# Delta * u of a scan unit loaded in three transfers of twelve channels instead of six of six

## The chip, the cores and the metric

The kernel runs on one core of one Trainium2 chip. The metric is the device time of one execution in microseconds (us); the figure for the kernel before is the median of three runs.

## What is computed

The reference has four layers on an image batch `x` of shape (4, 64, 64, 96). Layers 0 and 1 are selective-scan layers (a state-space block with a 3x3 depthwise convolution), layers 2 and 3 are linear attention followed by a feed-forward net with an FP8/FP16 quantisation. The change lies in the scan of layers 0 and 1, which is this recurrence for each of 4 images, 4 scan directions `k`, 192 channels `e` and 16 states `n`, over 4096 positions:

```python
dA = jnp.exp(d[..., None] * A)                       # d = delta of this position, A = -exp(A_logs)
h  = dA * h + d[..., None] * b[:, :, None, :] * u[..., None]
y  = jnp.einsum('bken,bkn->bke', h, c)
```

`d * u` does not depend on the state `n`; `b` and `c` do not depend on the channel `e`. So a kernel that holds states on partitions must bring the same `d * u` to 16 partitions.

## The kernel before

Each scan layer is run for two image pairs, which makes four phases. A phase has three parts: `prepare` (normalisation, projection, convolution, and the inputs of the scan, written to DRAM), `scan_phase` (the recurrence), and `finish` (gate, norm and output projection), where `finish` of one phase runs beside `prepare` of the next. Layers 2 and 3 follow at the end.

**Layout of the scan.** The 128 partitions hold 8 (image, direction) groups times 16 states. Partition `p` belongs to quarter `p // 32` of the 32-partition quarters, to group `p // 4 % 8`, and within it to one of 4 states. The time axis is cut into 8 chunks of 512 positions (`NC`, `TC`), the channels into 16 blocks of 12 (`NEB`, `EB`). One chunk of one block is a *unit*: a tile `h` of 128 partitions x 12 channels x 512 positions in float32, four of which are in rotation (`bufs=4`). A phase has 128 units, in the order chunk by chunk and block by block, so that four phases have 512.

**What a unit needs.** `load` (L381) first issues `load_delta` (L371), which brings delta, split into three bfloat16 parts, into 24 partitions (`dlt`). Then `load_quarters` (L391) fills the tile `h` with delta * u, straight from DRAM: each of the 8 group rows is read four times (a broadcast of stride zero), once for each of the 4 states of a quarter. To feed four quarters there are two copies of the array `du` in DRAM. With `first` counting quarters, the three combinations in the loop of L387 are:

- `first=1, quarters=2`: the two middle quarters (64 partitions), from both copies. Below it is called **A**.
- `first=0, quarters=1`: the first quarter (32 partitions), from copy 0. Called **B**.
- `first=3, quarters=1`: the last quarter (32 partitions), from copy 1. Called **C**.

Each is issued twice, for channels 0 to 5 and for channels 6 to 11, so the order of a unit's transfers is dlt, A0, A1, B0, B1, C0, C1. A row of `du` is padded by two channels (`PITCH`), and the channels of a block lie one behind the other in it, so the source of one partition is one contiguous run of 6 x 512 x 4 = 12,288 bytes.

**What is done with it.** GpSimd multiplies `h` by `b`, three channels at a time (`times_b`, L403, four for a unit, begun half a unit ahead: `B_LEAD`). TensorE spreads delta to 128 partitions through a 0/1 matrix (`replicate`, L408), ScalarE takes the exponential of it in PSUM (`decay`, L414), VectorE runs the recurrence along time, one channel at a time (`scan`, L420, twelve for a unit, in place in `h`). One unit later TensorE contracts the states with `c` (`contract`, L432), ScalarE copies the result out of PSUM (`evict`, L449), and `store` (L457) writes it to DRAM with four small transfers (`y<-d`).

**Order.** The order on each engine in `scan_phase` is the order of the code (a manual schedule). All loads and stores of the scan are issued by SyncE (SP), one after another: at the end of unit `at` it issues the four stores of unit `at-1`, then in some units four small transfers of `b` or `c` (L344), then the load of unit `at+3` (L529 to L534). The waits are set by the framework. Every DMA takes one of eight completion semaphores in turn, and before it is issued SP waits until the DMA that used this semaphore before, eight DMAs back, has landed. An ordinary unit issues 11 DMAs (dlt, six of delta * u, four stores).

Of the kernel before, what the change touches and what calls it, by code (L numbers as in the profile page):

```python
# [32 lines left out]
EB = 12  # L33
# [47 lines left out]
class Consts:  # L81
# [3 lines left out]
    def load(self, pool, name, shape):  # L85
        t = pool.tile(shape, F32, name=name)
        self.nc.sync.dma_start(t, self.a[name])
        return t
# [39 lines left out]
class Scans:  # L128
# [19 lines left out]
    def prepare(self, ph):  # L148
# [16 lines left out]
        with self.tc.tile_pool(name="prep", bufs=1) as wp, self.tc.tile_pool(  # L165
# [3 lines left out]
            def load(name, shape, at=0):  # L169
                t = wp.tile([at + shape[0]] + shape[1:], F32, name=name)  # L170
                nc.sync.dma_start(t[at:], a[pre + name])
                return t

            xp = load("x_proj", [C, 2, 2, XD2])
            dt_w = load("dt_w", [XD2 - 2 * NS, 2, E], at=2 * NS)
            conv_b = load("conv_b", [C, 2])
            ds = load("Ds", [C, 2, K])
            dsum = wp.tile([C, 2], F32, name="dsum")
# [202 lines left out]
    def load(self, u):  # L381

        nc, ph = self.nc, u.ph
        u.h = self.units.tile([128, EB, TC], F32, name="h", bufs=4)
        self.load_delta(u)
        n = EB // 2
        for first, quarters in ((1, 2), (0, 1), (3, 1)):  # L387
            for e in range(0, EB, n):
                self.load_quarters(u, e, n, first, quarters)

    def load_quarters(self, u, e, n, first, quarters):  # L391

# [591 lines left out]
```

## Time and profile before

| quantity | value |
|---|---|
| median of 3 runs | 12483.71 us (12462.94 to 12492.15) |
| profiled execution, its own time | 12443.48 us |
| its span, first to last instruction | 12441.7 us |
| the four scan stretches, first to last scan instruction | 774.8 to 2684.3, 3613.3 to 5524.1, 6462.3 to 8374.4, 9306.6 to 11235.0 us |
| busy in the span: PE, VectorE, ScalarE, GpSimd | 81%, 75%, 58%, 59% |
| TensorE clock granted | 0.665 |

The profile is of one execution. A group of instructions is named by its line, engine, operation and tiles; behind the bar stand its busy time, the mean duration of one in ns, and the idle time of its engine just before it with what ended most of that. `SPq` is SyncE's queue; its entries are the issuing of DMAs, not the moving of the data. The data moves on 16 DMA engines, and the share that the profile gives is a mean over the 16.

### The profile page before, as it was taken

What the parts mean: (1) busy time and instruction counts of PE and PEld (TensorE: products, weight loads), DVE (VectorE), ACT (ScalarE), POOL (GpSimd) and SP (SyncE); (2) the same over time, 40 slices, a digit from 0 to 9 for tenths busy, and PEclk for the clock granted to TensorE, in tenths of its full rate; (3) what the DMA queues carried; (4) which work ended last, traced back from release to release, by engine and by line L of the source; (5) the groups of instructions that cost most, each with busy time, mean ns of one, the idle gap of its engine ahead of it and who ended that gap; (6) DMA issues with size and microseconds to landing.
All of it is one profiled execution on the core that took longest, in us unless ns stands there. A gap on an engine that the chain in (4) does not pass through costs nothing.

```text
span 12441.7 us, 340858 instructions
## 1 busy us (share of the span) xinstructions
PE 10107.0 (81%) x147008; PEld 4972.1 (40%) x147008; DVE 9376.9 (75%) x9235; ACT 7185.6 (58%) x11815; POOL 7386.0 (59%) x2316
## 2 busy tenths in 40 slices
PE   7758888879878888879878888888878888887777
PEld 2224444433334444433334444443334444444333
DVE  2479999963569999982469999992459999993567
ACT  2456666644456666653456666663446666662556
POOL 0159999950149998960139899880129989990000
PEclk8665565669675555659775656558776655557787
DMA  3567676754667676764566777664567666663110
GB/s 92 172 227 247 244 248 247 248 168 140 213 205 246 245 247 244 250 200 128 176 215 244 246 247 249 243 226 125 174 202 249 244 243 245 245 244 122 30 21 11
DMA packets 882704, 2491.45 MB, mean 200 GB/s; under 512 B 279058, under 2 KB 561840, under 8 KB 737456
## 3 DMA queue, kind: packets, MB, share of 16 engines
q1 hardware_dynamic: 552496, 2163.38, 50.6%
q10 hardware_dynamic: 328704, 306.26, 8.5%
q8 instruction: 1158, 18.97, 0.7%
q14 instruction: 346, 2.83, 0.1%
HBM read 1955.42 MB, written 513.80 MB: 198 GB/s over the span
## 4 chain that ended last, share of the span: by engine, by line
DMA 53%; PE 20%; SPq 8%; DVE 7%; ACT 4%; issue 4%; POOL 3%; ACTq 1%; POOLq 0%; DVEq 0%
DMA h<-du 47%; PE c L260 8%; SPq L396 7%; POOL h L406 3%; PE f L591 2%; DVE h L423 2%; PE d L306 2%; DMA yk<-y 1%; PE c L289 1%; PE f L600 1%; POOL parts L320 1%; PE f L682 1%; DMA du<-du_sb 1%; PE y L441 1%; DVE parts L321 1%
## 5 line engine op out<-in xcount | busy, mean ns | idle before, releaser
L406 POOL TENSOR_TENSOR h<-h,b 128x1536 f32<-128x1536 f32 x2048 | 7016.6, 3456 | 780.6 <-DMA h<-du 369.0
L423 DVE TENSOR_TENSOR_SCAN h<-a,carry,h 128x512 f32<-128x512 f32 x5376 | 6356.7, 1259 | 391.8 <-POOL h L406 360.9
L416 ACT ACTIVATE a<-a,a_col 128x512 f32<-128x512 f32 x6144 | 4030.3, 662 | 1966.6 <-PE a L412 1814.4
L441 PEld LDWEIGHTS y<-h,cw 128*32 128x32 f32 x131072 | 2886.3, 145 | 3597.6 <-issue 1606.1
L441 PE MATMUL y<-h,cw 128*32 128x48 f32 x131072 | 3702.1, 269 | 438.0 <-ACT a L416 216.9
L412 PE MATMUL a<-dlt,rep 24*128 24x512 bf16 x6144 | 3319.4, 551 | 884.8 <-DVE h L423 782.1
L320 POOL CAST parts<-dl 96x1024 bf16<-96x1024 f32 x256 | 341.3, 1348 | 3092.1 <-DVE dl L317 2785.6
L316 DVE TENSOR_TENSOR du_sb<-dl,xc 96x1024 f32<-96x1024 f32 x256 | 397.3, 1577 | 1296.2 <-ACT dl L314 1234.8
L453 ACT COPY d<-y 128x384 f32<-128x384 f32 x2048 | 979.6, 478 | 485.7 <-PE y L441 432.7
L260 PE MATMUL c<-xn,taps 96*96 96x512 f32 x2304 | 1034.1, 609 | 73.5 <-DVE xn L245 71.0
L423 DVE TENSOR_TENSOR_SCAN h<-a,h 128x512 f32<-128x512 f32 x768 | 869.6, 1201 | 189.0 <-ACT a L416 110.6
L412 PEld LDWEIGHTS <-rep 24*128 24x128 bf16 x6144 | 471.9, 101 | 903.6 <-issue 451.0
L306 PE MATMUL d<-xd,dt_w 7*96 7x512 f32 x1024 | 520.8, 859 | 254.9 <-ACT xd L292 225.6
L260 PEld LDWEIGHTS c<-xn,taps 96*96 96x96 f32 x2304 | 382.6, 167 | 707.5 <-issue 628.7
L823 POOL MEMSET tn<- 1x4096 f32 x8 | 27.8, 3506 | 865.0 <-PE pa L843 514.7
L267 ACT ACTIVATE xc<-c,conv_b 96x512 f32<-96x512 f32 x128 | 87.3, 682 | 718.1 <-PE c L260 633.2
L591 PE MATMUL f<-yk,perm 128*128 128x384 f32 x1024 | 415.9, 546 | 99.6 <-DMA yk<-y 88.8
L314 ACT ACTIVATE dl<-d 96x1024 f32<-96x1024 f32 x256 | 252.0, 1017 | 400.9 <-DMA delta<-parts 234.5
L321 DVE TENSOR_TENSOR parts<-dl,parts 96x1024 bf16<-96x1024 f32 x256 | 366.9, 1455 | 153.2 <-POOL parts L320 153.1
L289 PE MATMUL c<-xc,x_proj 96*103 96x512 f32 x512 | 420.2, 958 | 4.2 <-ACT xc L267 4.2
L306 PEld LDWEIGHTS d<-xd,dt_w 7*96 7x96 f32 x1024 | 151.7, 212 | 542.4 <-ACT xd L292 295.8
L360 ACT ACTIVATE cw<-c,gmask 128x256 f32<-128x256 f32 x512 | 287.9, 573 | 126.2 <-DMA h<-du 65.9
(114 smaller groups left out, 5650.6 us busy)
## 6 DMA issues: line engine op xcount, KB each, us to landing
h<-du SPq DMA_DIRECT2D x1024, 768.0 KB
h<-du SPq DMA_DIRECT2D x2048, 384.0 KB
delta<-parts ACTq DMA_DIRECT2D x512, 288.0 KB
dlt<-delta SPq DMA_DIRECT2D x512, 288.0 KB
du<-du_sb SPq DMA_DIRECT2D x256, 384.0 KB
du<-du_sb ACTq DMA_DIRECT2D x256, 384.0 KB
y<-d SPq DMA_DIRECT2D x2048, 48.0 KB
yk<-y SPq DMA_DIRECT2D x256, 384.0 KB
```

The lines of the kernel that those rows point to most:

```text
L260: nc.tensor.matmul(rows(ps[:C]), taps[:, tap, h * C : (h + 1) * C], xn[:, ROWS * c + dy : ROWS * (c + 1) + dy, dx : dx + HW], start=tap == ...
L289: nc.tensor.matmul(rows(ps[:XD2]), xp[:, k, h], u[:, h], start=h == 0, stop=h == 1)
L306: nc.tensor.matmul(ps[:, m], dt_w[part, k, m * C : (m + 1) * C], xd[part], start=True, stop=True)
L321: nc.vector.tensor_tensor(parts[:, 2], delta, parts[:, 1], ALU.subtract)
L396: self.nc.sync.dma_start(u.h[32 * first : 32 * (first + quarters), e : e + n].rearrange("p e t -> p (e t)"), source.rearrange("a g e t -> ...
L406: self.nc.gpsimd.tensor_tensor(h, h, b, ALU.mult)
L412: self.nc.tensor.matmul(u.a[n], rep, u.dl[:, n], start=True, stop=True)
L416: self.nc.scalar.activation(u.a[n], u.a[n], AF.Exp, scale=u.ph.a_col[:, at : at + 1])
L423: self.nc.vector.tensor_tensor_scan(u.h[:, n], u.a.pop(n), u.h[:, n], 0.0 if u.c == 0 else u.ph.carry[:, at : at + 1], ALU.mult, ALU.add,)
L441: self.nc.tensor.matmul(view(u.y[32 * j : 32 * j + 32], l2 * EB, (8 * EB, 4), (1, EB)), u.ph.cw[u.c][:, l1, 8 * j + l2], view(u.h, 64 * l1 ...
L453: self.nc.scalar.copy(u.d[:, :, :, l1], u.y[:, : 32 * EB].rearrange("p (t h x) -> p t h x", t=4, h=2))
L591: nc.tensor.matmul(ps[:, : 4 * C].rearrange("p (w v e) -> p w v e", w=4, v=nv), cst.perm[:, k], view(t, off, (sw if k < 2 else -sw, 4), (1 ...
```

## The change

The inner loop over halves of six channels goes, and `load_quarters` is called with all twelve channels at once. A unit's transfers are now dlt, A, B, C: three of delta * u with contiguous runs of 24,576 bytes, in place of six with runs of 12,288. The bytes, the partitions and the order of the quarters are the same. An ordinary unit now issues 8 DMAs. Nothing else differs in the code.

```diff
         u.h = self.units.tile([128, EB, TC], F32, name="h", bufs=4)
         self.load_delta(u)
-        n = EB // 2
         for first, quarters in ((1, 2), (0, 1), (3, 1)):
-            for e in range(0, EB, n):
-                self.load_quarters(u, e, n, first, quarters)
+            self.load_quarters(u, 0, EB, first, quarters)
```

`load_quarters(u, e, n, first, quarters)` itself is unchanged; it loads `n` channels from channel `e` on.

## The prediction

> **What bounds the kernel now.** I read the page's chain first, then the scan stretches by windows, then one stretch as a timeline and as a chain. The page says where to look:
>
> ```profile
> DMA h<-du 47%; PE c L260 8%; SPq L396 7%; POOL h L406 3%; PE f L591 2%; DVE h L423 2%; PE d L306 2%; DMA yk<-y 1%; PE c L289 1%; PE f L600 1%; POOL parts L320 1%; PE f L682 1%; DMA du<-du_sb 1%; PE y L441 1%; DVE parts L321 1%
> L406 POOL TENSOR_TENSOR h<-h,b 128x1536 f32<-128x1536 f32 x2048 | 7016.6, 3456 | 780.6 <-DMA h<-du 369.0
> L423 DVE TENSOR_TENSOR_SCAN h<-a,carry,h 128x512 f32<-128x512 f32 x5376 | 6356.7, 1259 | 391.8 <-POOL h L406 360.9
> ```
>
> More than half of the chain is this load and its issue; VectorE waits for GpSimd, GpSimd for the load. The windows of the first scan stretch:
>
> ```profile
> core 0: us, PE busy (x) PEld busy (x) DVE busy (x) ACT busy (x) POOL busy (x), PEclk, DMA share, GB/s
> 775.00:2684.00 1909.00, 1621.64 (x34042) 832.57 (x34041) 1805.52 (x1536) 1305.54 (x2268) 1740.52 (x508) 0.60 0.70 245
> ```
>
> VectorE is busy 1806 of 1909 us: about 103 us a phase are lost. DMA at 0.70 looks free; it isn't, as shown below. The timeline of VectorE in a steady stretch, and then the chain of waits there (start, us, what):
>
> ```profile
> 1534.08 14.21 DVE L423 TENSOR_TENSOR_SCAN h<-a,carry,h 128x512 f32<-128x512 f32 x12 [0.34 <-POOL h L406]
> 1548.71 14.21 DVE L423 TENSOR_TENSOR_SCAN h<-a,carry,h 128x512 f32<-128x512 f32 x12 [0.42 <-POOL h L406]
> ```
>
> ```profile
> 1520.83 12.44 DMA h<-du
> 1533.29 0.69 SPq L396
> ...
> 1535.42 12.72 DMA h<-du
> 1548.14 0.02 issue
> 1548.16 0.69 SPq L396
> ```
>
> A unit needs 14.21 us of VectorE but begins every 14.6 to 14.7 us. The chain repeats: C1 lands (1533.27), which lets SP issue B0 (eight DMAs on), three more issues, and C1 of the next unit lands at 1548.14. The waits of SP say the same:
>
> ```profile
> SPq L396 <- DMA h<-du: 2039.9, 1326, 4.0
> SPq L461 <- DMA h<-du: 633.0, 657, 2.8
> ```
>
> Is this loop a latency or a full resource? The trace's semaphore records, which have the landing of each DMA engine's share, answer it. A shows 16 landings, B and C show 8 and one at the issue. So B, C and dlt run on 8 engines only, the same ones; the other 8 carry halves of A and stores. In one unit the last landings are dlt 1550.75, A0 1552.35, A1 1554.21, B0 1556.04, B1 1557.88, C0 1559.73, C1 1562.88. Four packets of 12,288 B in 1.84 us is 461 ns each; the packet records have 462 ns. The loaded engines ("low eight") have no gap. Over 508 units the median of C1 to C1 is 14.72 us: stores and dlt 2.70, A0 1.60, A1 1.85, B0 1.85, B1 1.84, C0 1.85, C1 2.85. Only C1 is 1.0 us over its 1.85. It is then that the high eight start A0 of the next unit: A0 is issued 4.6 us before C1 lands, its packets start 1.2 us later, the high eight finish A0 at +1.1 and A1 at +3.2, taking 6.6 us for 8 packets that need 3.7. Where no A runs beside it (before a load of b or c) C1 takes 1.85. The two streams slow each other. So the bound is the low eight engines, 14.72 us a unit, of which some 1.2 us (1.0 in C1, about 0.2 in dlt and stores) is contention.
>
> [...]
>
> **The change, part by part.**
>
> *Longer packets.* Packet medians in steady scans: 768 B 36 ns, 2048 B 84 ns, 12,288 B 462 ns. The line through these is 8.6 ns + bytes / 27.1 per ns. A 24,576 B packet should take 914 ns in place of 924. A low engine carries 24 of the short ones a unit (8 of A, 8 of B, 8 of C), so 12 x 8.6 = 0.10 us go. Three completion writes fewer, about 10 ns each by the 4 B packets: 0.03. Together -0.14 us a unit (rounded up). No packet in this trace is over 16,384 B, so an unseen split could make it 0; the bounds are -0.14 and 0.
>
> *SP.* Three issues of 0.65 us fewer a unit. SP stands in waits, so this is worth nothing itself.
>
> *The semaphore waits move.* With 8 DMAs a unit and 8 semaphores, each waits for its own counterpart of the unit before: A for A, C for C. A is now held by the later of two things. First, SP's order: the last eviction of a unit starts 12.4 us after its first scan (1513.77 against 1501.35), four stores take 2.5 and dlt 0.7, and the scan starts 3.5 after C lands (one GpSimd multiply): 3.5 + 12.9 + 3.2 = 19.6 us after the landing of a unit three back, which is 2 x 14.7 - 19.6 = 9.8 us before C of the unit just ahead lands. Second, the landing of A ahead: 4 x 1.84 + 1.2 = 8.6 us before. So A is issued some 8.6 us before the landing of C where it was 4.6 us. The low eight have work queued either way and gain nothing.
>
> *Contention.* But the high eight now begin A at -7.4 and, at 6.6 us, end at -0.8: 2.9 us of it lie beside B and 3.7 beside C, none beside dlt and stores, which cost little. Before, 3.4 us lay beside C0 and C1. Price beside C: 1.0 / 3.4 = 0.3 us per us, hence 1.1. Price beside B: the trace has it only at each phase's start, where the third load follows at once. There A0 ran beside B0 (1.85, no loss) and A1 beside B1 (2.85, 3.45, 3.00, 2.40 in the four phases); over 8.1 us of A the units lost 1.4 on average, 0.17 per us. So 2.9 us cost 0 to 1.0. The new loss is 1.1 to 2.1; I take 1.6. Against 1.2 that is +0.4; the bounds are -0.2 (all at 0.17 per us and some relief from one start of A in place of two) and +0.9.
>
> *Later first multiply.* GpSimd's first multiply waited for C0 and now waits for all of C, 1.84 us later. Behind it stand its own three multiplies, then VectorE's scans, and one unit on TensorE's contraction. In a loop set by DMA rate this shifts the phase, once: 4 x 1.84 = +7 us. At a phase's start it is hidden: VectorE's first scan there waits 37.73 us for ScalarE, whose 16 weights wait for c behind this load.
>
> *Sum.* -0.14 + 0.38 = +0.24 us a unit, over 496 units (the first four of a phase are ahead of the DMA): +119, with the +7, +126 us on the profiled 12443.5 (span 12441.7 and 1.8 around it), 1.0%. The profiled execution is 40 us below the median shown; on the median the same ratio gives 12,610 us.
>
> The units in which four transfers of b or c stand before the load keep their gap of about 2.6 us: there the fourth still waits for the last C, before and after.
>
> **Rivals.** *Packets decide* (28%): contention stays at 1.2 us wherever A lies, as the phase starts suggest (1.4 in all). Then -0.14 x 496 + 7 = -62 us: 12,420. Against it: units where A0 was early by chance (issued 7 us ahead of C1's landing) have C0 at 3 to 4.3 and C1 at 2.8 to 3.7. For it: part of that is another delay, also seen without A (single transfers of 3.4), which itself makes A look early.
>
> *Contention eases* (7%): one long A per unit starts once, not twice, and the streams fall out of each other's way, as where A ran on all 16 from a standstill with packets back at 462 ns. The floor is VectorE's 14.21 us a unit: 0.5 us x 496 = -250, near 12,240.
>
> *No change that can be measured* (8%): the two terms cancel or the packets are split; 12,460 to 12,508.
>
> *Contention doubles* is the far end of my forecast: +0.9 - 0.14 = +0.76 us a unit, +380 us, 12,870.
>
> **How the numbers follow.** The forecast, more contention than the packets save, has 57%, its own range 12,510 to 12,870. Below it lie 12,420 with 28%, 12,240 with 7%, and no change with 8%. About 0.2% (25 us) is what a measurement of this kernel can tell from none. The range 12,360 to 12,850 leaves out the 7% and the far ends. Faster 0.35, same 0.08, slower 0.57.
>
> **What would show it.** In the profile after: 24,576 B packets near 914 ns on the quiet low eight; SP's waits for h<-du at L394 fall, because A is issued earlier; if I am right, B plus C take more than 8.4 us from A's landing to C's (the sum now: 1.85 + 1.84 + 1.85 + 2.85 = 8.4), stores plus dlt less than 2.7, and VectorE waits longer for GpSimd than 391.8 us. I am wrong if units begin every 14.6 us or less, or if A is still issued 4 to 5 us ahead of C's landing.

## The result, and the profile after

| | before | after |
|---|---|---|
| median of 4 runs each, us | 12480.49 (12462.94 to 12492.15) | 13659.6 (13646.34 to 13677.61) |
| ratio, 95% interval | | 1.0947 [1.0927, 1.0967] |
| span of the profiled execution | 12441.7 | 13675.8 |
| the four scan stretches | 1909.5, 1910.9, 1912.1, 1928.4 | 2237.3, 2225.6, 2211.9, 2205.7 |
| one unit, start to start (medians of the four stretches) | 14.64 to 14.81 | 17.27 to 17.54 |

The kernel became 9.5% slower. The forecast was 12,610 us with a range up to 12,850: the direction was right, the size was too small by a factor of nine (+126 us against some +1,180). The stretches add up to 8880.5 us against 7660.9, so 1219.6 of the 1234.1 us by which the span grew lie in the scan.

From the page of the kernel after, the chain by line and the groups of GpSimd and VectorE (busy, mean ns of one, then idle before it and what ended most of that):

```profile
DMA h<-du 54%; PE c L260 7%; DVE h L421 5%; PE f L589 2%; POOL h L404 2%; PE d L306 2%; DMA yk<-y 1%; PE c L289 1%; PE y L439 1%; DMA y<-d 1%; PE f L680 1%; PE f L669 1%; PE f L598 1%; POOL parts L320 1%; DMA delta<-parts 1%
L404 POOL TENSOR_TENSOR h<-h,b 128x1536 f32<-128x1536 f32 x2048 | 7003.2, 3451 | 2018.4 <-DMA h<-du 1159.2
L421 DVE TENSOR_TENSOR_SCAN h<-a,carry,h 128x512 f32<-128x512 f32 x5376 | 6360.6, 1260 | 1472.3 <-POOL h L404 1404.6
```

The work itself costs what it did: a scan takes 1260 ns (1259 before), a multiply 3451 (3456). Only the idle time grew, VectorE's from 391.8 to 1472.3 us and GpSimd's from 780.6 to 2018.4. The chain is the same load as before. It has lost `SPq` as a member, as the chain of waits in the steady stretch shows (start, us, what):

```profile
1509.17 18.04 DMA h<-du
1527.22 0.02 issue
1527.23 17.39 DMA h<-du
1544.63 0.02 issue
1544.64 17.30 DMA h<-du
```

C of a unit is issued when C of the unit before lands, and lands 17.3 us later. Nothing but transfers lies between. VectorE in the same stretch, as a timeline, stops before every unit:

```profile
1530.87 14.21 DVE L421 TENSOR_TENSOR_SCAN h<-a,carry,h 128x512 f32<-128x512 f32 x12 [3.88 <-POOL h L404]
1548.28 14.21 DVE L421 TENSOR_TENSOR_SCAN h<-a,carry,h 128x512 f32<-128x512 f32 x12 [3.21 <-ACT d L451]
1565.59 14.21 DVE L421 TENSOR_TENSOR_SCAN h<-a,carry,h 128x512 f32<-128x512 f32 x12 [3.10 <-POOL h L404]
```

The stops were 0.34 and 0.42 us before. The windows of the scan stretch show the puzzle that the experiments had to solve (columns as before):

```profile
775.00:3011.00 2236.00, 1693.10 (x34042) 849.67 (x34041) 1806.76 (x1536) 1320.34 (x2267) 1739.44 (x509) 0.52 0.69 209
```

The DMA engines are as busy as before, 0.69 against 0.70, yet they move 209 GB/s in place of 245. They are occupied and slow.

**The landings.** The semaphore records give the landing of each DMA engine's share. The table is worked out from them as in the prediction: medians in us over some 450 units of a run without a load of b or c; each column is the time from the landing of the transfer before, taken at the last engine. "A issued" is against the landing of the last transfer of the unit ahead, and "upper done" is when the high eight engines have finished their half of A, on the same scale. Which half of A that is, partitions 64 to 95 (below called A's upper half), is taken from the order of the source rows, an assumption of the author's that the bare transfers further down agree with.

| kernel | stores + dlt | A | B | C | unit | A issued | upper done |
|---|---|---|---|---|---|---|---|
| before | 2.66 | 1.59 + 1.85 | 1.85 + 1.84 | 1.85 + 2.88 | 14.67 | -4.68 | +3.18 |
| after | 2.87 | 3.40 | 4.82 | 6.11 | 17.32 | -10.97 | -0.97 |

B should take four packets of 0.914 us, 3.7 us, and so should C. They take 4.8 and 6.1. A is issued 11 us ahead, so the high eight work on it from before C begins (-6.11) to 0.97 us before C ends.

The packets say how. On quiet engines a packet of 24,576 bytes takes 912 to 921 ns, as predicted. The packets that start between 1519 and 1523 us run on all sixteen engines at once, and each takes 1,862 to 1,936 ns: twice as long. Following one low engine by the ends and starts of its packets, A and B of a unit take 914 to 921 ns each, and the four of C 1244, 1859, 1884 and 1900.

### The profile page after: what moved, and what is told of

Same layout as the page of the kernel before. It is cut to its first block, busy times and chain, and to the rows that moved or that the text cites. A ratio compares the mean times of both kernels' runs of the same rounds, so it can differ in the third digit from the quotient of the medians.

```text
span 13675.8 us, 337834 instructions
## 1 busy us (share of the span) xinstructions
PE 10384.2 (76%) x147008; PEld 5048.7 (37%) x147008; DVE 9382.3 (69%) x9235; ACT 7234.3 (53%) x11815; POOL 7373.0 (54%) x2316
## 4 chain that ended last, share of the span: by engine, by line
DMA 60%; PE 19%; DVE 9%; ACT 4%; issue 4%; POOL 3%; SPq 1%; ACTq 1%; POOLq 0%; DVEq 0%
DMA h<-du 54%; PE c L260 7%; DVE h L421 5%; PE f L589 2%; POOL h L404 2%; PE d L306 2%; DMA yk<-y 1%; PE c L289 1%; PE y L439 1%; DMA y<-d 1%; PE f L680 1%; PE f L669 1%; PE f L598 1%; POOL parts L320 1%; DMA delta<-parts 1%
## 5 line engine op out<-in xcount | busy, mean ns | idle before, releaser
L404 POOL TENSOR_TENSOR h<-h,b 128x1536 f32<-128x1536 f32 x2048 | 7003.2, 3451 | 2018.4 <-DMA h<-du 1159.2
L421 DVE TENSOR_TENSOR_SCAN h<-a,carry,h 128x512 f32<-128x512 f32 x5376 | 6360.6, 1260 | 1472.3 <-POOL h L404 1404.6
L410 PE MATMUL a<-dlt,rep 24*128 24x512 bf16 x6144 | 3526.1, 582 | 1727.5 <-DVE h L421 1628.1
L439 PEld LDWEIGHTS y<-h,cw 128*32 128x32 f32 x131072 | 2927.4, 148 | 3951.6 <-issue 1950.6
L439 PE MATMUL y<-h,cw 128*32 128x48 f32 x131072 | 3756.6, 269 | 562.6 <-ACT a L414 252.6
```

What stands on the lines that cost most here:

```text
L404: self.nc.gpsimd.tensor_tensor(h, h, b, ALU.mult)
L410: self.nc.tensor.matmul(u.a[n], rep, u.dl[:, n], start=True, stop=True)
L421: self.nc.vector.tensor_tensor_scan(u.h[:, n], u.a.pop(n), u.h[:, n], 0.0 if u.c == 0 else u.ph.carry[:, at : at + 1], ALU.mult, ALU.add,)
L439: self.nc.tensor.matmul(view(u.y[32 * j : 32 * j + 32], l2 * EB, (8 * EB, 4), (1, EB)), u.ph.cw[u.c][:, l1, 8 * j + l2], view(u.h, 64 * l1 ...
```

## The experiments

**A cause to test.** About half the rate on both sides (1,862 to 1,936 ns a packet, 912 to 921 when quiet) looks like one shared resource. The theory of the halves, at this point an assumption of the author's, says where it lies: two streams slow each other if the partitions that they write to are in the same half, 0 to 63 or 64 to 127, and do not if they are in different halves. C writes 96 to 127; the half of A that the high eight engines carry writes 64 to 95: the same half. B and the lower half of A write to the other one. Two more suspects were DRAM (the copy that is read) and plain contention of any two streams, which was the prediction's own model. Where an expectation compares these causes, the forecast of the theory of the halves stands first.

The runs up to the one with four copies are single ones, each beside a run of the kernel before.

**C from the other copy.** In the kernel after, C reads copy 0 of `du` like B, so that it doesn't read the copy that A's upper half reads.

```diff
-        copies = slice(0, 2) if quarters == 2 else slice(first % 2, first % 2 + 1)
+        copies = slice(0, 2) if quarters == 2 else slice(0, 1)
```

> The kernel after, with C reading copy 0 of du instead of copy 1, so that only A's upper half reads copy 1. [...] nothing changes there, about 13,660 us, C still 5.3 us between the mean landings of the eight engines. DRAM theory (both streams read the same rows of copy 1): the slowing goes, 12,300 to 12,500 us, C about 3.7 us. Any-two-streams theory (16 engines at once are slow whatever they do, or long packets are): about 13,660 us.

Measured 13720.43 us, beside 12520.14 for the kernel before on the same chip; a unit takes 17.5 us. Against the 13659.6 us of the kernel after nothing changed that a single run can show. That both read the same copy in DRAM is not it.

**Other quarters.** In the kernel after, A goes to quarters 0 and 1, then come 2 and 3. Now both single quarters use the upper partitions (64 to 127), and A's upper half (32 to 63) lies in the other half.

```diff
-        for first, quarters in ((1, 2), (0, 1), (3, 1)):
+        for first, quarters in ((0, 2), (2, 1), (3, 1)):
```

> The kernel after, with the quarters dealt out otherwise: A fills partitions 0 to 63, B 64 to 95 (copy 0), C 96 to 127 (copy 1). The same bytes, copies, engines, semaphores and order. [...] low eight engines run at full rate, a unit falls to what VectorE needs (14.2 us), 12,150 to 12,400 us, below the kernel before. DRAM theory: A's upper half and C still read copy 1, about 13,660 us. Any-two-streams theory: about 13,660 us.

Measured 13172.54 us, units of 15.8 to 16.3: between the 12,150 to 12,400 of the theory of the halves and the others' 13,660. It recovers some 40% of the loss. The last transfer falls from 6.11 to 5.32 us, the middle one from 4.82 to 3.66. But A's upper half now lies in the same half of the partitions as A's own lower half: low engines that have finished their unit are already in the next dlt and A (partitions 0 to 31), and the packets of 24,576 bytes that start between 1509 and 1511.4 us take 2,011 to 2,360 ns. The conflict was moved and made shorter, not removed; that this is all of what was missed is not shown. One reading doesn't fit: a third packet of C on one engine took 2,147 ns beside an upper half of A that went to the other half of the partitions.

**C ahead of B.** In the kernel before, so that the six-channel transfers that lie beside A's upper half are those of B.

```diff
-        for first, quarters in ((1, 2), (0, 1), (3, 1)):
+        for first, quarters in ((1, 2), (3, 1), (0, 1)):
```

> The kernel before (six transfers), with C issued ahead of B: the order is A0, A1, C0, C1, B0, B1. A of the next unit is issued when C1 lands and runs beside B1. [...] the last transfer of a unit takes 1.85 us instead of 2.85 and the time falls to 12,150 to 12,400 us. DRAM theory: B reads copy 0, A's upper half copy 1, so it falls as well. Any-two-streams theory: 12,480 us as before.

Measured 12671.00 us against 12520.14: slower, where the halves alone ask for a gain (12,150 to 12,400). The last transfer did get shorter, 2.49 us in place of 2.88, but 1.85 is what it needs, and a unit takes 15.46 by its last landings. So with no half in common the last transfer still loses 0.64 us, of 1.03 before. A's upper half starts slowly (its first packets take 1.1 us in the median and up to some 1.6, in place of 0.46; in the kernel before it is 1.2 and some 1.6), and for about four microseconds most packets of both halves of A take 570 to 900 ns. One low engine falls behind the rest. The halves don't explain that, and it was not settled.

**A in one piece, B and C in two; and the reverse.** Both from the kernel before. The first has ten DMAs a unit, the second nine.

```diff
-        n = EB // 2
         for first, quarters in ((1, 2), (0, 1), (3, 1)):
+            n = EB if quarters == 2 else EB // 2
```

> A in one transfer of twelve channels, B and C in two of six: five transfers, ten DMAs a unit, so A waits on the semaphore of B1 of the unit ahead, as A0 does in the kernel before. If the early issue of A is what costs (it was issued 10.9 us ahead of C's landing after, 4.6 before), this one is near the kernel before, 12,400 to 12,600 us, though A has the long packets. If the long packets of A cost in themselves, 12,900 us or more.

```diff
-        n = EB // 2
         for first, quarters in ((1, 2), (0, 1), (3, 1)):
+            n = EB // 2 if quarters == 2 else EB
```

> The other half of the change alone: A in two transfers of six channels, B and C each in one of twelve; nine DMAs a unit. A0 then waits for the semaphore of A1 of the unit ahead and is issued as early as in the kernel after, A1 for B's. Issue theory (A too early, beside C): slow, 13,000 to 13,700 us. If only the whole A made it slow: about 12,500 us.

Measured 12514.96 us for the first (12520.14 beside it) and 13538.12 for the second (12453.59 beside it). VectorE's scans on their pages, the first kernel and then the second:

```profile
L424 DVE TENSOR_TENSOR_SCAN h<-a,carry,h 128x512 f32<-128x512 f32 x5376 | 6361.3, 1261 | 461.4 <-POOL h L407 445.6
```

```profile
L424 DVE TENSOR_TENSOR_SCAN h<-a,carry,h 128x512 f32<-128x512 f32 x5376 | 6361.3, 1260 | 1327.4 <-POOL h L407 1228.5
```

This pair splits the change. The long A costs nothing that a single run can show. With ten DMAs the DMA eight before A is B1 of the unit ahead, and A is issued at -4.80, as before. With nine it is A1 of the unit ahead: A is issued at -10.99, and the loss is nearly whole, although A still comes in two pieces. What decides is how early A may go, and that is set by the number of DMAs against eight semaphores.

**C, A, B.** The kernel after with C first, so that A's upper half lies beside C of its own unit.

```diff
-        for first, quarters in ((1, 2), (0, 1), (3, 1)):
+        for first, quarters in ((3, 1), (1, 2), (0, 1)):
```

> The kernel after with its three transfers in the order C, A, B. A of the next unit, issued when A of this one has landed, now runs on the upper eight engines beside B (partitions 0 to 31) and the stores, no longer beside C. [...] the 1.6 us that C lost come back, units of 15 us or less, 12,300 to 12,900 us. If the two streams slow each other whatever they write (a limit of what 16 engines read together): 13,300 us or more.

Measured 13201.15 us (12453.59 beside it), units of 15.8 to 15.9. That lies between the two ranges, so neither theory has the size right. A is issued at -4.41 and its upper half is done at +5.57. By the mean of the low engines C takes 5.58 us, B 3.83: C, now at the front of the unit, loses 1.9 us, and B, at its end, 0.17. The slow transfer is again the one that writes 96 to 127.

**The transfers alone.** The kernel before, with bare transfers put ahead of all phases: A to partitions 32 to 95 or to 0 to 63, four of each kind, first alone and then behind two transfers of 32 partitions on the low eight (to 0 to 31, or to 96 to 127).

```diff
+        for low in (None, 0, 3):
+            for first in (1, 0):
+                for r in range(4):
...
+                    if low is not None:
+                        move(tk[0], low, 1, slice(low % 2, low % 2 + 1), at)
+                        move(tk[1], low, 1, slice(low % 2, low % 2 + 1), at + EB)
+                    move(ta, first, 2, slice(0, 2), at + 2 * EB)
```

> The kernel before with a stretch of bare transfers of du put in front (no engine computes there), four of each kind, so its time means nothing; the landings do. [...] a lone transfer of 64 partitions and 24 KB runs takes about 3.7 us on the engines to partitions 32 to 63 and 64 to 95, and about 7.3 us to partitions 0 to 63[...]. With two transfers like C (96 to 127) ahead on the lower eight engines the upper half of A to 64 to 95 needs about 7.3 us, with two like B (0 to 31) about 3.7 us; for A to 0 to 63 it is the other way round. DRAM-limit theory: all of these between 5 and 6 us, whatever the partitions.

The time of this kernel, 12915.03 us, contains the added transfers and says nothing. A small store (`mseen<-mta`) waits for each A, so SP's timeline can be read directly. An A alone to 32 to 95, and an A alone to 0 to 63:

```profile
106.18 0.56 SPq L903 DMA_DIRECT2D mta<-mdu  x1
112.83 0.21 SPq L918 DMA_DIRECT2D mseen<-mta  x1
...
136.94 0.53 SPq L903 DMA_DIRECT2D mta<-mdu  x1
147.12 0.21 SPq L918 DMA_DIRECT2D mseen<-mta  x1
```

6.65 us and 10.18 us for the same bytes from the same rows on the same sixteen engines: 3.5 us more, near the 3.7 us that the data need alone by the estimate above (four packets of 0.914 us). An A to 32 to 95 behind two transfers to 0 to 31, then behind two to 96 to 127:

```profile
191.16 0.58 SPq L903 DMA_DIRECT2D mta<-mdu  x1
203.99 0.22 SPq L918 DMA_DIRECT2D mseen<-mta  x1
...
314.69 0.58 SPq L903 DMA_DIRECT2D mta<-mdu  x1
330.90 0.22 SPq L918 DMA_DIRECT2D mseen<-mta  x1
```

12.83 and 16.21 us. The landings from the semaphore records, in us after the issue of each, complete it (the very first A, which also waited for its data, is left out):

| two transfers ahead, then A | the two ahead, last engine | A, upper half |
|---|---|---|
| none, A to 32-95 | | 5.9 to 6.8 (all sixteen engines) |
| none, A to 0-63 | | 8.9 to 10.3 (all sixteen engines) |
| to 0-31, A to 32-95 | 6.9 to 7.0 and 9.9 to 10.1 | 6.8 to 7.2 |
| to 0-31, A to 0-63 | 8.7 to 8.9 and 13.3 to 13.4 | 10.4 to 11.0 |
| to 96-127, A to 32-95 | 8.3 to 9.0 and 13.1 to 13.5 | 10.4 to 10.9 |
| to 96-127, A to 0-63 | 6.7 to 7.1 and 9.8 to 10.1 | 6.7 to 7.1 |

Only the pairs in the same half of the partitions slow each other, and both sides lose: the second of the two ahead lands some 3.3 us later, A's upper half some 3.7. Their packets take about 1,900 ns while both run. In the other pairs sixteen engines run at full rate (912 ns) with the same source rows, so here it is not DRAM, nor contention as such. The theory of the halves agrees with these times; what in the hardware the partitions of a half have in common is not shown. The price is now measured: for as long as both run, a packet takes about 1,900 ns in place of 912.

**One transfer of four quarters.** Four copies of `du` in DRAM, and one DMA of 128 partitions for a unit.

```diff
-                self.dram.tile([2, G, E + PITCH, TC], F32, name="du", bufs=2 * NC) for _ in range(NC)
+                self.dram.tile([4, G, E + PITCH, TC], F32, name="du", bufs=2 * NC) for _ in range(NC)
...
-            for copy, queue in enumerate((nc.scalar, nc.sync)):
+            for copy, queue in enumerate((nc.scalar, nc.sync, nc.scalar, nc.sync)):
...
-        for first, quarters in ((1, 2), (0, 1), (3, 1)):
-            self.load_quarters(u, 0, EB, first, quarters)
+        self.load_quarters(u, 0, EB, 0, 4)
...
-        copies = slice(0, 2) if quarters == 2 else slice(first % 2, first % 2 + 1)
+        copies = slice(first, first + quarters)
```

> Four copies of du in DRAM in place of two, so that a unit's delta * u is one transfer of 128 partitions, with 32 source rows on all 16 engines. If the bound is the lower eight engines and what they share with A, the load takes some 7.5 to 10 us of 16 engines a unit and the scan falls to VectorE's 14.2 us a unit, 112 us a phase less than before; writing two more copies (about 200 MB) costs in the preparation, between nothing and 4 x 100 us. So 12,050 to 12,500 us. If 16 engines reading are limited in all to the 250 GB/s seen, the scan stays at 14.6 us a unit or more, 12,500 to 12,900 us.

VectorE's scans on its page:

```profile
L420 DVE TENSOR_TENSOR_SCAN h<-a,carry,h 128x512 f32<-128x512 f32 x5376 | 6317.4, 1256 | 0.0
```

No idle time at all in these scans: with the load spread over both halves and all sixteen engines the scan stretches are VectorE's own work, 1793.4 us each, 487 us less in sum than before. (Engines and halves change together here, so this run does not tell them apart.) But DRAM writes rise from 514 to 715 MB, all in the preparation, and the whole takes 12513.48 us (12453.59 beside it). About 550 us are given back outside the stretches, where 0 to 400 were expected.

**The DMA count put right, in two ways.** If the number of DMAs decides, the long transfers can be kept and A held back by the count alone. First, the kernel after with two loads of one element that nothing reads, which makes ten DMAs a unit and puts C eight ahead of A.

```diff
+        self.spare = [pool(f"spare{i}", 1).tile([1, 1], F32, name=f"spare{i}") for i in range(2)]
...
+        for spare in self.spare:
+            nc.sync.dma_start(spare, self.a["one_row"][:1])
```

> The kernel after, its three transfers unchanged, with two loads of 4 bytes behind them that nothing reads. They only move the semaphores on: with ten DMAs a unit A of the next unit waits for C of this one to land, so its upper half runs beside the stores, dlt and A's own lower half[...] C falls from 5.3 to about 3.7 us, a unit's load from 16.5 to about 13.2 us, VectorE's 14.2 us becomes the bound, 12,130 to 12,350 us, faster than the kernel before. If the length of the transfers itself is what costs, 13,400 us or more.

Second, the kernel after with C in three pieces of four channels. That is ten DMAs too, and the first third of C stands eight ahead of A.

```diff
         for first, quarters in ((1, 2), (0, 1), (3, 1)):
-            self.load_quarters(u, 0, EB, first, quarters)
+            n = EB // 3 if first == 3 else EB
+            for e in range(0, EB, n):
+                self.load_quarters(u, e, n, first, quarters)
```

> The kernel after with C in three transfers of four channels, also ten DMAs a unit: A waits for the first third of C, is issued 2.4 us ahead of C's end and starts 1.2 us later. [...] about 1.2 us of sharing a unit in place of all of C, so between the kernel with two spare loads and the one before, 12,200 to 12,500 us. If the length of the transfers costs, 13,000 us or more.

| kernel | time, us | ratio to before | stores + dlt | A | B | C | unit | A issued |
|---|---|---|---|---|---|---|---|---|
| two spare loads | 12448.91 | 0.9992 [0.9983, 1.0002] | 2.52 | 4.76 | 3.39 | 3.70 | 14.39 | +0.08 |
| C in thirds | 12204.36 | 0.9797 [0.9781, 0.9813] | 2.90 | 3.41 | 3.65 | 1.24 + 1.24 + 1.32 | 14.08 | -2.51 |

(Medians of 12 and of 4 runs; the kernel before beside them: 12459.68 us, 15 runs.) Two tiny loads take away all of the 9.5%. C is back at 3.70 us. But there A is issued only when C has landed, the low eight engines run dry, and A takes 4.76 us: the gap of about one microsecond goes with the gain that was expected (12,130 to 12,350 us) and did not come. With C in thirds A goes 2.5 us ahead, enough to cover its own start (1.5 us from its issue at 1515.25 to its first packet in the kernel after) and too late to lie beside much of C. From its page, the groups:

```profile
L406 POOL TENSOR_TENSOR h<-h,b 128x1536 f32<-128x1536 f32 x2048 | 7020.0, 3460 | 518.5 <-DMA h<-du 268.7
L423 DVE TENSOR_TENSOR_SCAN h<-a,carry,h 128x512 f32<-128x512 f32 x5376 | 6335.2, 1258 | 182.9 <-POOL h L406 177.3
```

and VectorE's timeline:

```profile
1520.76 28.31 DVE L423 TENSOR_TENSOR_SCAN h<-a,carry,h 128x512 f32<-128x512 f32 x24 [0.87 <-POOL h L406]
1549.24 11.86 DVE L423 TENSOR_TENSOR_SCAN h<-a,carry,h 128x512 f32<-128x512 f32 x10 [0.17 <-POOL h L406]
```

Two units run through without a stop. The stretches are 1859.6, 1858.3, 1841.9 and 1845.8 us, 255 less in sum than before, and the time fell by 255. This version beats both kernels, by 2.0% (1.9 to 2.2%) and by 10.7% (12204.36 against 13659.6). It also has the longer packets. What they add to it is not shown: no run holds A back in the same way with packets of 12,288 bytes.

## Why the prediction was right or wrong

**The step that failed** is the price of contention: "Price beside C: 1.0 / 3.4 = 0.3 us per us, hence 1.1", and with it "The new loss is 1.1 to 2.1; I take 1.6." The mechanism named was the right one: A is issued earlier, and its upper half then lies beside B and C. The price was taken from a kernel in which the overlap is short, as if it were a constant tax for each microsecond. In the kernel after, the last engine loses 3.6 us a unit over the 3.7 that B and C need each: 2.4 in C and 1.2 in B.

The loss in C is a halving that lengthens its own overlap. A's upper half lies beside C from -6.11 to -0.97, 5.1 us in place of the 3.7 of the prediction, and half of 5.1 is 2.6, near the 2.4: some 0.5 us per us, not 0.3. The loss in B is just over the upper bound that the prediction gave it (1.0). That is no confirmation, since B has no half in common with A's upper half. It sits on an engine that runs late (the eight shares of C land 8.4 us apart in the median, 3.7 before), whose packets of B also took 1,182 to 1,862 ns; that part is open. With these two terms the prediction's sum is 3.6 - 1.2 - 0.14 = +2.3 us a unit, 496 times, some +1,120 us, where the stretches grew by 1,220. The pace is that of the last engine, because C of the next unit is issued when its share lands: by the mean of the eight low engines C takes 5.30 us and B 3.88.

Why the kernel before showed only 0.3 us per us is not settled either. The halves alone don't make it: with B as the last transfer 0.64 of the 1.03 us remained, and the prediction's own reading of the phase starts has B1 at 2.40 to 3.45 us beside an A1 whose upper half goes to the other half.

The other steps:

- *Longer packets*: right. 914 ns predicted, 912 to 914 measured. The long A alone changed nothing that a single run can show (12514.96 against 12520.14).
- *The semaphore waits move*: the rule was right, "A for A, C for C". The size, 8.6 us ahead, was 10.97, because A waits for A to land and B and C then took 10.93 (4.82 + 6.11), not 4 x 1.84 + 1.2. This number follows from the price above.
- *SP*: that its issues are worth nothing was right. That its waits at L394 would fall was wrong. From the waits of SP, two lines of the kernel before (beside the 2039.9 and 633.0 us of the prediction) and then the kernel after:

```profile
SPq L376 <- DMA h<-du: 571.3, 450, 2.8
SPq L344 <- DMA h<-du: 277.5, 227, 2.9
```

```profile
SPq L394 <- DMA h<-du: 5106.1, 1309, 7.7
SPq L344 <- DMA h<-du: 440.4, 166, 4.7
```

  After, these two come to 5546.5 us; before, the four lines come to 3521.7. SP stands where the loop is slow, whatever is slow in it; the sum was no test of the issue time.
- *Later first multiply*: nothing contradicts its +7 us, and nothing here measures it.
- *Stores and dlt under 2.7 us*: they took 2.87 at the last engine. No gain there. B plus C over 8.4 us from A's landing: right, 10.93.
- *Rivals*: "packets decide" and "contention eases" both needed a contention that doesn't grow with the overlap; it grew from 1.0 to 3.6 us a unit. "Contention doubles" had the right direction, and its +0.76 us a unit was still under a third of the 2.65 that came (17.32 against 14.67), because its upper bound was the worst reading of the same rate.
- *What is shared*: the prediction has a price beside C and one beside B, and no cause for either. Reading C from another copy changed nothing that a single run can show (13720.43 us against 13659.6), and in the bare transfers the same source rows took 6.65 us or 10.18 by the partitions that they went to.

## What to carry to other kernels

Where two transfers can be in flight together, write down which partitions each engine's share goes to: in the bare transfers shares in the same half (0 to 63, or 64 to 127) halved each other's rate (about 1,900 ns a packet in place of 912), and shares in different halves didn't. In the full kernel different halves were not always free of loss (B as the last transfer kept 0.64 us). When DMAs are merged and completion semaphores are handed out in turn, count again which DMA stands eight ahead of each: the merge moves issue times, and that can cost far more than longer packets bring (here A went from 4.68 us ahead to 10.97 and a unit from 14.67 us to 17.32, where the longer packets were to save 0.14). A slowing measured at a small overlap is not a rate: ask which resource is shared, and let both streams lengthen the overlap.

## What was not expected of the hardware

- Sixteen DMA engines moved less than eight would have alone: while both streams wrote to the same half, a packet of 24,576 bytes took some 1,890 ns on each of sixteen, 208 GB/s in sum by these figures, where eight at 914 ns move 215.
- Streams in different halves were slowed too while others shared one (1,182 to 1,862 ns for packets of B, 2,147 for one of C with the quarters changed), though the bare transfers never showed it. It was not tried what couples them. One thing that may make an engine late, though none of this shows that it does, stands in both traces: the queue q8, which the profile calls instruction, moves a packet of 16,384 bytes about every 7 us before and 8 us after, which takes some 1.1 us. By the ends and starts of packets, one (1,018 ns from 1515.11 us) falls on the low engine whose packets of 1,182 and 1,862 ns follow. No run took these packets away.
- Two loads of a single element in each unit moved the time by 8.9% (13659.6 to 12448.91).
- The granted TensorE clock was 0.613 after, 0.665 before, 0.767 with C ahead of B. It did not set the time: of twelve runs with two spare loads one had 0.782 and took 12457.98 us, the others had 0.679 to 0.691 and took 12425.44 to 12478.27.
